# The last layer of a two-layer convolution block: a third tile of x by channels, asked for two units ahead, and residual rows asked for in their own unit

## The chip, the cores and the metric

The kernel runs on one core of one Trainium2 chip. A core has five engines that run beside each other, each with its own queue of instructions: TensorE (PE in the profile, its weight loads PEld) multiplies matrices, VectorE (DVE) and ScalarE (ACT) work on the elements, GpSimd (POOL) and SyncE (SP) do little here but issue DMA transfers. The engines wait for each other through semaphores. The metric is the time of one execution in microseconds (us); lower is better.

## What is computed

The input x has 48 channels of 256 x 256 pixels. The program runs two layers, each with a group normalisation `_gn` ahead of it and a residual sum behind it:

```python
# --- layer 0: attention over 4 x 4 patches, 8 heads ---
x = x + _L0_conv_ref(_gn(x), w_qkv, w_dw, temperature, w_proj)
# --- layer 1: this case is about this one ---
x = x + _L1_conv_ref(_gn(x), Ws, Hs, Cs, 64)

def _L1_conv_ref(x, Ws, Hs, Cs, window_size):
    B, C, H, W = x.shape
    ws = window_size                                   # 64
    xb = x.reshape(B, C, H // ws, ws, W // ws, ws)
    out = jnp.einsum('bcphqw,twW,thH,tcC->bCpHqW', xb, Ws, Hs, Cs)
    return out.reshape(B, C, H, W)
```

In layer 1 the picture is cut into 16 windows of 64 x 64 pixels. In each window, three terms t are added up, and in each term the data are multiplied by a 48 x 48 matrix over the channels, a 64 x 64 matrix over the columns of the window and a 64 x 64 matrix over its rows.

## The kernel before

Layer 0 takes the larger part of the program. It ends with a projection (lines 697 to 757), which writes its result with the residual added, 48 channels of 256 x 256 floats, to the tensor `x1s` in DRAM (L731), and works out the statistics that layer 1's normalisation needs. The normalisation is folded into the channel matrix `csn` and a bias `cbias`.

Layer 1 follows at L760. Its work is cut into eight units (L773): a unit is a strip of 64 rows by 128 columns, that is two windows side by side. The unit is worked through in these steps:

- `unit_load(u)` (L777) issues four DMAs on SyncE's queue. Two fetch the x tile `xq` ("lxq" in the profile, L784): channels on the partitions, once for the upper and once for the lower 32 rows of the strip. Two fetch the residual rows `rt` ("lrt", L787): image rows on the partitions, 24 channels each. Each of the four moves 768 KB in pieces of 512 bytes. Both kinds have two buffers (`bufs=2` of the pools `lx`, L760, and `lr`, L761).
- `over_c(u)` (L793) multiplies the x tile by the channel matrices, three image rows at a time, in 11 steps (L804: PSUM tile `pa`, two buffers). VectorE subtracts the bias and writes the product to `zt` ("lzt", L811). It is a generator: it stops after each step, and the caller decides when the next one is issued. A step takes a matmul for the upper and one for the lower half tile for each image row.
- `over_w(u, c0, c1)` (L819) multiplies by the column matrices for eight of the channels (L826: PSUM tile `pb`), and ScalarE copies the result to `yt` ("lyt", L833).
- `over_h(u, q)` (L836) multiplies by the row matrices and adds the three terms up in one PSUM tile `pc` (L843), which has a single buffer.
- `residual(u, q, pc)` (L852) lets VectorE add `pc` to the residual rows in place (L855). GpSimd then issues two stores of 256 KB from there to the output (L858). So a buffer of residual rows comes free when the last stores of its unit have landed.

The loop (L865 to L884) stands under `tc.manual_schedule()`: every engine gets its instructions in just the order in which the program text issues them. A unit has three parts q. Each part has two `over_w`, and behind each of them two steps of `over_c` of the unit after it. `over_h` runs one part late: that of part q of unit u is issued in the part that follows, and that of the last part in the first part of the next unit. `unit_load(u + 1)` stands at the head of unit u. SyncE computes nothing, so it takes the DMAs one after the other, as soon as the semaphores that each of them needs allow. A tile may be overwritten when all that read its buffer before have finished, and the framework puts the waits for that ahead of the DMA.

In the profile, TensorE's matmuls in fp32 are counted twice, so a call of `over_w` has 48 records where the text has 24.

Of the kernel before, what the change touches and what calls it, by code (L numbers as in the profile page):

```python
# [43 lines left out]
def conv_preact_kernel(  # L44
# [343 lines left out]
    with tc.tile_pool(name="xn", bufs=1) as xnp, tc.tile_pool(name="cst", bufs=1) as cst, tc.tile_pool(  # L388
        name="nps", bufs=2, space=PSUM
# [75 lines left out]
    with tc.If(nc.values_load(large) > 0):  # L465
# [8 lines left out]
        with tc.tile_pool(name="mk", bufs=NM) as mk, tc.tile_pool(name="mq", bufs=2) as mq, tc.tile_pool(  # L474
            name="mps", bufs=2, space=PSUM
# [23 lines left out]
    with tc.tile_pool(name="ahead", bufs=2) as ah, tc.tile_pool(name="ae", bufs=3) as ae, tc.tile_pool(  # L499
        name="asm", bufs=6  # L500
# [196 lines left out]
    with tc.tile_pool(name="pj", bufs=3) as pj, tc.tile_pool(name="pjs", bufs=1) as pjs, tc.tile_pool(  # L697
        name="pps", bufs=3, space=PSUM
# [58 lines left out]
        nc.vector.tensor_copy(cbias, pb1)  # L757


    with tc.tile_pool(name="lx", bufs=2) as lx, tc.tile_pool(name="lz", bufs=2) as lz, tc.tile_pool(  # L760
        name="lr", bufs=2  # L761
    ) as lr, tc.tile_pool(name="ly", bufs=4) as ly, tc.tile_pool(name="ps1", bufs=2, space=PSUM) as ps1, tc.tile_pool(
        name="ps2", bufs=2, space=PSUM
    ) as ps2, tc.tile_pool(name="ps3", bufs=1, space=PSUM) as ps3:
        wsb = lz.tile([128, T3, 128], F32, name="wsb", bufs=1)
        nc.vector.memset(wsb, 0.0)
        hsb = lz.tile([128, T3, WS], F32, name="hsb", bufs=1)
        for s in range(2):
            r = slice(s * WS, (s + 1) * WS)
            nc.scalar.dma_start(out=wsb[r, :, r], in_=Ws.rearrange("t w v -> w t v"))  # L770
            nc.scalar.dma_start(out=hsb[r], in_=Hs.rearrange("t h g -> h t g"))
        HW = WS // 2
        units = [(yw, xh) for yw in range(H // WS) for xh in range(2)]  # L773
        NQ = 3
        xqs, rts, zts, blks, parts = {}, {}, {}, {}, {}

        def unit_load(u):  # L777

            yw, xh = units[u]
            xcol = slice(xh * 128, (xh + 1) * 128)  # L780
            xq = lx.tile([64 + C, HW, 128], F32, name="lxq")
            for s in range(2):
                y0 = yw * WS + s * HW
                nc.sync.dma_start(out=xq[s * 64 : s * 64 + C], in_=x1s[:, y0 : y0 + HW, xcol])  # L784
            rt = lr.tile([128, NQ * 8, 128], F32, name="lrt")
            for s in range(2):
                nc.sync.dma_start(  # L787
                    out=rt[s * WS : (s + 1) * WS],
                    in_=x1s[s * 24 : (s + 1) * 24, yw * WS : (yw + 1) * WS, xcol].rearrange("c y x -> y c x"),
                )  # L790
            xqs[u], rts[u] = xq, rt

        def over_c(u):  # L793

            xq = xqs[u]
            zt = zts[u] = lz.tile([128, T3 * C, WS], F32, name="lzt")
            zv = zt.rearrange("p k (s y) -> p s y k", s=2)
            for y0 in range(0, HW, 3):
                n = min(3, HW - y0)
                pa = ps1.tile([128, 2, 512], F32, name="pa")  # L800
                for i in range(n):
                    for s in range(2):
                        r = slice(s * 64, s * 64 + C)
                        nc.tensor.matmul(  # L804
                            pa[:, s, i * T3 * C : (i + 1) * T3 * C],
                            lhsT=xq[r, y0 + i, :],
                            rhs=csn[r],
                            start=True,
                            stop=True,
                        )  # L810
                nc.vector.tensor_tensor(  # L811
                    zv[:, :, y0 : y0 + n, :],
                    pa[:, :, : n * T3 * C].rearrange("p s (y k) -> p s y k", y=n),
                    cbias.rearrange("p (u v k) -> p u v k", u=1, v=1).to_broadcast([128, 2, n, T3 * C]),
                    ALU.subtract,
                )
                yield

        def over_w(u, c0, c1):  # L819

            yt = ly.tile([128, T3, 512], F32, name="lyt")
            for t in range(T3):
                pb = ps2.tile([128, 4, 128], F32, name="pb2")
                for i in range(4):
                    for s, c in enumerate((c0, c1)):
                        nc.tensor.matmul(  # L826
                            pb[s * WS : (s + 1) * WS, i, :],
                            lhsT=zts[u][:, t * C + c + i, :],
                            rhs=wsb[:, t, :],
                            start=True,  # L830
                            stop=True,
                        )
                nc.scalar.copy(yt[:, t, :], pb.rearrange("p i x -> p (i x)"))  # L833
            return yt

        def over_h(u, q):  # L836

            pc = ps3.tile([128, 2, 512], F32, name="pc")
            for t in range(T3):
                for b in range(2):  # L840
                    for s in range(2):
                        r = slice(s * WS, (s + 1) * WS)
                        nc.tensor.matmul(  # L843
                            pc[b * WS : (b + 1) * WS, s, :],
                            lhsT=hsb[r, t, :],
                            rhs=parts[u, q][b][r, t, :],
                            start=(t == 0),
                            stop=(t == T3 - 1),
                        )
            residual(u, q, pc)  # L850

        def residual(u, q, pc):  # L852
            yw, xh = units[u]
            rv = rts[u][:, q * 8 : (q + 1) * 8, :].rearrange("p i x -> p (i x)")
            nc.vector.tensor_add(rv, pc.rearrange("p b n -> p (b n)"), rv)  # L855
            for s in range(2):
                c0 = s * 24 + q * 8
                nc.gpsimd.dma_start(  # L858
                    out=oc[c0 : c0 + 8, yw * WS : (yw + 1) * WS, xh * 128 : (xh + 1) * 128].rearrange("c y x -> y c x"),
                    in_=rts[u][s * WS : (s + 1) * WS, q * 8 : (q + 1) * 8, :],  # L860
                )

        with tc.manual_schedule():  # L865
            unit_load(0)
            for _ in over_c(0):
                pass
            late = None
            for u in range(len(units)):  # L870
                if u + 1 < len(units):
                    unit_load(u + 1)
                ahead = over_c(u + 1) if u + 1 < len(units) else iter(())
                for q in range(NQ):
                    parts[u, q] = []
                    for b in range(2):
                        c0 = b * 24 + q * 8
                        parts[u, q].append(over_w(u, c0, c0 + 4))
                        for _ in range(2):
                            next(ahead, None)  # L880
                    if late:
                        over_h(*late)
                    late = u, q
            over_h(*late)  # L884
# [41 lines left out]
```

## Time and profile before

| | us |
|---|---|
| median of 3 runs | 3835.93 (3830.28 to 3836.73) |
| the profiled execution | 3845.87 |
| its span, from the first to the last instruction | 3844.1 |
| first DMA of layer 1 to the end of the span | 3495.7 to 3844.1: 348.4 |

In layer 1, by the groups of instructions from 3495 us on:

| line, engine | what | busy us | count | mean ns |
|---|---|---|---|---|
| L826 PE | over_w | 147.9 | 2304 | 287 |
| L804 PE | over_c | 95.1 | 1024 | 333 |
| L843 PE | over_h | 67.3 | 576 | 598 |
| L811 DVE | bias, lzt | 136.3 | 88 | 1621 |
| L833 ACT | lyt | 84.3 | 144 | 586 |
| L855 DVE | residual | 29.4 | 24 | 1225 |

A line of the page or of an answer names the source line (L826), the engine, the operation, the tile written and the tiles read (`pb<-wsb,lzt`), and a count. "idle before" is time in which the engine stood still just ahead of the instruction, with the instruction or transfer that released it. The chain of waits goes back from the last instruction of the program, at each step to what released it or to the instruction before it on its engine; time that stands in the chain is time that sets the end. A DMA on SyncE's queue (SPq) is shown with the time of its issue, not with that of its data.

### The profile page before, as it was taken

What the parts mean: (1) busy time and instruction counts of PE and PEld (TensorE: products, weight loads), DVE (VectorE), ACT (ScalarE), POOL (GpSimd) and SP (SyncE); (2) the same over time, 40 slices, a digit from 0 to 9 for tenths busy, and PEclk for the clock granted to TensorE, in tenths of its full rate; (3) what the DMA queues carried; (4) which work ended last, traced back from release to release, by engine and by line L of the source; (5) the groups of instructions that cost most, each with busy time, mean ns of one, the idle gap of its engine ahead of it and who ended that gap; (6) DMA issues with size and microseconds to landing.
All of it is one profiled execution on the core that took longest, in us unless ns stands there. A gap on an engine that the chain in (4) does not pass through costs nothing.

```text
span 3844.1 us, 99863 instructions
## 1 busy us (share of the span) xinstructions
PE 3525.9 (92%) x44216; PEld 2927.6 (76%) x44216; DVE 2199.1 (57%) x3520; ACT 1717.9 (45%) x2668; POOL 583.3 (15%) x535
## 2 busy tenths in 40 slices
PE   1856999999999999999999999999999999755998
PEld 0324777788888888888888888888888888514776
DVE  5562776169727962994399359826972222365553
ACT  0223565555545544554455455545554444200222
POOL 0150212012201220221022112201220000000111
PEclk9877999999999999999999999999999999866999
DMA  6475676534523443444244325433542000598555
GB/s 142 153 163 144 178 196 179 175 109 117 119 81 101 119 110 87 104 120 98 83 117 115 94 81 128 111 88 92 128 113 75 24 18 22 116 238 141 111 105 100
DMA packets 280235, 441.66 MB, mean 115 GB/s; under 512 B 57354, under 2 KB 205082, under 8 KB 276336
## 3 DMA queue, kind: packets, MB, share of 16 engines
q1 hardware_dynamic: 225150, 260.52, 26.7%
q0 software_dynamic: 48896, 165.90, 19.2%
q10 hardware_dynamic: 5746, 8.73, 1.0%
q8 instruction: 351, 5.75, 0.6%
q14 instruction: 92, 0.75, 0.1%
HBM read 234.76 MB, written 199.95 MB: 113 GB/s over the span
## 4 chain that ended last, share of the span: by engine, by line
PE 73%; issue 10%; DMA 8%; DVE 2%; SPq 1%; POOL 0%; ACT 0%; POOLq 0%; ACTq 0%; DVEq 0%
PE big L339 32%; PE big L570 31%; DMA lxq<-x1s 3%; PE pb L826 3%; PE pa L804 2%; PE big L183 2%; DMA pot<-os__70 2%; PE pc L843 1%; DMA qkv<-o 1%; DMA pxt<-in_x_dram 1%; PE pst L524 1%; PE pt L587 1%; PE pn L253 1%; DMA xs<-in_x_dram 1%; DMA kt<-qkv 1%
## 5 line engine op out<-in xcount | busy, mean ns | idle before, releaser
L541 ACT ACTIVATE e<-big,nmx 128x1024 f32<-128x1024 f32 x1024 | 1144.0, 1117 | 846.2 <-PE big L339 636.4
L339 PE MATMUL big<-kt,qt 128*128 128x512 f32 x6144 | 1441.9, 394 | 57.9 <-DMA kt<-qkv 54.9
L570 PEld LDWEIGHTS big<-vn,e 128*64 128x64 f32 x32768 | 1364.8, 137 | 87.7 <-ACT e L541 45.1
L570 PE MATMUL big<-vn,e 128*64 128x96 f32 x32768 | 1422.7, 248 | 9.1 <-ACT ot L186 4.0
L339 PEld LDWEIGHTS big<-kt,qt 128*128 128x128 f32 x6144 | 1147.9, 189 | 322.0 <-issue 63.1
L581 DVE TENSOR_TENSOR oacc<-big,oacc 128x768 f32<-128x768 f32 x480 | 458.2, 955 | 708.7 <-PE big L570 708.7
L234 DVE SCALAR_TENSOR_TENSOR acc<-pad,dwt,acc 126x1024 f32<-126x1024 f32 x600 | 779.3, 1300 | 34.2 <-ACT acc L215 18.5
L292 POOL TENSOR_TENSOR ol<-o,oh 126x1024 fp32r<-126x1024 f32 x80 | 189.9, 2373 | 909.1 <-DVE ss L249 810.1
L554 DVE TENSOR_REDUCE zt<-zs 128x1 f32<-128x4 f32 x256 | 38.8, 152 | 368.5 <-ACT e L541 368.5
L811 DVE TENSOR_TENSOR lzt<-pa,cbias 128x864 f32<-128x864 f32 (+1 forms) x88 | 136.3, 1621 | 134.5 <-PE pa L804 134.5
L541 ACT ACTIVATION_READ_ACCUMULATOR e<-big,nmx 128x1 f32 x1024 | 196.3, 192 | 0.0
L833 ACT COPY lyt<-pb 128x512 f32<-128x512 f32 x144 | 84.3, 586 | 250.0 <-PE pb L826 250.0
L297 POOL DMA_DIRECT2D qkv<-o x80 | 101.0, 1262 | 567.8 <-DVE zu L556 348.7
L245 ACT ACTIVATE sq<-acc 126x1024 f32<-126x1024 f32 x75 | 79.3, 1058 | 171.7 <-issue 111.6
L279 DVE TENSOR_TENSOR o<-acc,y 126x1024 f32<-126x1024 f32 x75 | 149.4, 1992 | 11.0 <-DMA qkv<-o 11.0
L826 PEld LDWEIGHTS pb<-wsb,lzt 128*64 128x64 f32 x2304 | 132.1, 143 | 28.1 <-issue 21.1
L715 PE MATMUL pps<-pot,wp 96*96 96x512 f32 x128 | 77.9, 778 | 77.6 <-DMA pot<-os__70 77.6
L826 PE MATMUL pb<-wsb,lzt 128*64 128x128 f32 x2304 | 147.9, 287 | 1.3 <-issue 1.3
L186 ACT ACTIVATE ot<-big,bias 108x1024 f32<-108x1024 f32 x64 | 71.0, 1112 | 147.8 <-PE big L183 68.2
L804 PE MATMUL pa<-csn,lxq 48*128 48x144 f32 x1024 | 95.1, 333 | 33.9 <-DMA lxq<-x1s 32.6
L590 POOL DMA_DIRECT2D os__70<-oo x64 | 32.6, 514 | 615.4 <-ACT oo L589 615.4
L715 PEld LDWEIGHTS pps<-pot,wp 96*96 96x96 f32 x128 | 26.9, 218 | 128.0 <-issue 126.4
(115 smaller groups left out, 1897.6 us busy)
## 6 DMA issues: line engine op xcount, KB each, us to landing
pad<-t SPq DMA_DIRECT2D x80, 761.9 KB
qkv<-o POOLq DMA_DIRECT2D x80, 504.0 KB, 6.9
qkv<-oh POOLq DMA_DIRECT2D x80, 504.0 KB, 7.4
qkv<-ol POOLq DMA_DIRECT2D x80, 504.0 KB, 9.1
t<-ot SPq DMA_DIRECT2D x128, 217.7 KB
qt<-qkv SPq DMA_DIRECT2D x176, 96.0 KB
xs<-in_x_dram SPq DMA_DIRECT2D x128, 96.0 KB
os__70<-oo POOLq DMA_DIRECT2D x64, 192.0 KB, 2.8
```

The costliest lines, as they stand in the source:

```text
L234: nc.vector.scalar_tensor_tensor(self.acc, self.pad[:, dy : dy + KS, dx : dx + W], dwt[:, self.h, tap : tap + 1], self.acc, ALU.mult, ALU.add,
L279: nc.vector.tensor_tensor(self.o.rearrange("p (a b) x -> p a b x", a=KS), self.acc.rearrange("p a (x b) -> p a b x", b=KS), self.y.rearran ...
L292: eng.tensor_sub(self.ol, self.o, self.oh.bitcast(F32))
L297: nc.gpsimd.dma_start(out=qkv[self.h][i].rearrange("j (c k) n -> (j c) k n", k=KK)[:, :, px], in_=self.o if i == 2 else (self.ol if i else ...
L339: nc.tensor.matmul(ps[:, i, :], lhsT=qt[:, r, q0 : q0 + 128], rhs=kts[2 * j + i][:, r // 2, :], start=(r == 0), stop=(r == 2),)
L541: nc.scalar.activation(e[:, j * 1024 : (j + 1) * 1024], ps.rearrange("p a b -> p (a b)"), AF.Exp, bias=nmx[:, b : b + 1], accum_out=zs[:, ...
L570: nc.tensor.matmul(ps[p : p + 64, j // 4, j % 4 * HD : (j % 4 + 1) * HD], lhsT=e[:, mb * 128 + p : mb * 128 + p + 64], rhs=vn, start=(i == 0),
L581: nc.vector.tensor_add(oaccs[h, k], ps[:, :, : 4 * HD], oaccs[h, k])
L715: nc.tensor.matmul(ps[:, i : i + 2, :], lhsT=wp, rhs=ot[:, ki * KS + i : ki * KS + i + 2, :], start=True, stop=True,)
L804: nc.tensor.matmul(pa[:, s, i * T3 * C : (i + 1) * T3 * C], lhsT=xq[r, y0 + i, :], rhs=csn[r], start=True, stop=True,)
L811: nc.vector.tensor_tensor(zv[:, :, y0 : y0 + n, :], pa[:, :, : n * T3 * C].rearrange("p s (y k) -> p s y k", y=n), cbias.rearrange("p (u v ...
L826: nc.tensor.matmul(pb[s * WS : (s + 1) * WS, i, :], lhsT=zts[u][:, t * C + c + i, :], rhs=wsb[:, t, :], start=True, stop=True,)
```

## The change

`unit_load` is cut in two. `load_x(u)` fetches the x tile, `load_rows(u)` the residual rows. The pool of x tiles gets three buffers. Ahead of the loop the x tiles of units 0 and 1 are asked for; at the head of unit u the rows of that unit are asked for, and after them the x tile of unit u + 2.

```diff
-    with tc.tile_pool(name="lx", bufs=2) as lx, tc.tile_pool(name="lz", bufs=2) as lz, tc.tile_pool(
+    with tc.tile_pool(name="lx", bufs=3) as lx, tc.tile_pool(name="lz", bufs=2) as lz, tc.tile_pool(
...
-        def unit_load(u):
+        def load_x(u):
 
             yw, xh = units[u]
             xcol = slice(xh * 128, (xh + 1) * 128)
...
                 nc.sync.dma_start(out=xq[s * 64 : s * 64 + C], in_=x1s[:, y0 : y0 + HW, xcol])
+            xqs[u] = xq
+
+        def load_rows(u):
+
+            yw, xh = units[u]
+            xcol = slice(xh * 128, (xh + 1) * 128)
             rt = lr.tile([128, NQ * 8, 128], F32, name="lrt")
...
-            xqs[u], rts[u] = xq, rt
+            rts[u] = rt
...
-            unit_load(0)
+            for u in range(2):
+                load_x(u)
             for _ in over_c(0):
                 pass
             late = None
             for u in range(len(units)):
-                if u + 1 < len(units):
-                    unit_load(u + 1)
+                load_rows(u)
+                if u + 2 < len(units):
+                    load_x(u + 2)
```

What is computed stays the same; so does the order of the instructions on TensorE, VectorE, ScalarE and GpSimd.

## The prediction

> **What bounds the kernel now.** I read the page first, to see where the last layer lies, then the chain of waits over its end, the timeline of TensorE there, the timeline of SyncE's queue, and that queue's waits. The page says that TensorE is busy for 92% of the span, so a change to one layer can only win what TensorE stands still there. In the chain of waits (start in us, length in us, what) the last layer begins with the first x tile and then goes on so:
>
> ```profile
> 3496.13 13.98 DMA lxq<-x1s
> ...
> 3564.83 2.86 PE pb L826 x48
> 3567.69 1.67 PE pa L804 x24
> ...
> 3587.95 17.98 DMA lxq<-x1s
> ...
> 3605.97 3.25 PE pa L804 x22
> 3609.22 3.91 PE pb L826 x48
> ...
> 3629.00 17.38 DMA lxq<-x1s
> ```
>
> The reader is to see that up to 3584 the chain is TensorE alone, and that from there an x transfer of 17 to 19 us stands in it once per unit (five times: x tiles 3 to 7). On TensorE's own timeline (start, length, what, and in brackets the idle time before it and its releaser) these are the beginnings of units 1 and 2:
>
> ```profile
> 3564.76 2.93 PE L826 MATMUL pb<-wsb,lzt 128*64 128x128 f32 x48
> ...
> 3599.17 2.93 PE L826 MATMUL pb<-wsb,lzt 128*64 128x128 f32 x48
> 3602.03 0.51 PE L804 MATMUL pa<-csn,lxq 48*128 48x144 f32 x2
> 3605.97 3.25 PE L804 MATMUL pa<-csn,lxq 48*128 48x144 f32 x22 [3.43 <-DMA lxq<-x1s]
> 3609.15 3.98 PE L826 MATMUL pb<-wsb,lzt 128*64 128x128 f32 x48
> ```
>
> One matmul over channels (two records) runs on the half tile that has landed, then TensorE waits for the other half. Why the tile is late stands on SyncE's queue (start, length of the issues, tile):
>
> ```profile
> 3529.30 6.71 SPq L784 DMA_DIRECT2D lxq<-x1s  x2
> 3582.85 1.51 SPq L787 DMA_DIRECT2D lrt<-x1s  x2
> 3584.48 8.18 SPq L784 DMA_DIRECT2D lxq<-x1s  x2
> 3624.14 1.49 SPq L787 DMA_DIRECT2D lrt<-x1s  x2
> 3625.74 7.32 SPq L784 DMA_DIRECT2D lxq<-x1s  x2
> ```
>
> and in that queue's waits from 3520 on (waiter, releaser: us in total, times, longest):
>
> ```profile
> SPq L787 <- DMA out_dram<-lrt: 207.4, 13, 35.6
> ```
>
> The x tile of unit 3 is asked for only after the residual rows (lrt) of unit 2 have been issued, and those stand in the queue until the stores of unit 0, which read the same one of two buffers, have landed. Its own buffer had been free since over_c(1) ended near 3562. It then needs until 3605.9, while unit 2 wants it at 3602.
>
> [...] no L784 issue between 3536.0 and 3584.48, although its buffer was free. [...] the granted clock is 1.00 in unit 1 and 0.92 in units 2 to 5, and after the 3.43 us gap 22 matmul records take 3.25 us where 24 take 1.67, and the next 48 take 3.98 where they take 2.93.
>
> **The change, part by part.** A unit begins at the first matmul of its first over_w. From TensorE's timeline, units 1 to 7 begin at 3564.76, 3599.17, 3640.07, 3680.77, 3722.28, 3763.50 and 3806.91. Unit 1, which never waits, takes 34.41 us; TensorE is busy in all of it. Units 2 to 6 take 40.90, 40.70, 41.51, 41.22 and 43.41, together 207.74. Unit 7 has no over_c and no x to wait for.
>
> 1. *The x tile is asked for one unit earlier.* After the change SyncE's queue reads: x0, x1, rows 0, x2, rows 1, x3, rows 2, x4, rows 3, x5 and so on. Rows 2 still wait for the stores of unit 0 (3582.85, or 18.1 us into unit 1), and what goes out behind them at 3584.5 is x4 instead of x3. X4 lands after the same 21.4 us (3605.9 - 3584.5), some 41 us into unit 1. Unit 3 wants it 2.9 us after it begins: with units of 34.41, at 71.7. Margin about 30 us. X3 stands ahead of rows 2, waits only for over_c(0) (over at 3529.3), and is in long before 3602. So the wait in units 2 to 6 goes, with the cold matmuls after it: 207.74 - 5 x 34.41 = 35.7 us. As a check: the waits shown for the x tile between 3560 and the end are 20.0 us on TensorE in 5, and the cold stretch costs (3.25 - 22/24 x 1.67) + (3.98 - 2.93) = 2.8 each, 14 in all; 34.0 together.
>
> 2. *The rows are asked for in their own unit.* In the queue only their place against x changes: their wait for the stores of two units before ends at the same instant. Rows u land at the latest with the burst, 40 us into unit u-1, that is 5 us into unit u; the first residual wants them after two over_w pairs and over_h, 20.9 + 2.7 = 23.6 us into it. Cost nothing; the cover is 18 us at least.
>
> 3. *The third x tile.* 16 KiB more in each partition, no instruction. The buffer asked for in unit u held x of u-1, whose last reader ran in unit u-2. No new wait.
>
> 4. *The start.* Behind x0 now comes x1 and not rows 0; four issues as before, and x1 is wanted at 3535.9, the rows at 3554. X0 took until 3510.1. From 3496 to 3510.1 about 1.95 MB moved (the windows of DMA rate), of which x0 is 1.57; the other 0.38 is what followed it and the small weights. If none of that were in the way, x0 would be in 0.38 MB / 140 GB/s = 2.7 us sooner; if twice as much came between, 2.7 later. I take 0 and keep both ends.
>
> 5. *What is late next.* In a unit of 34.4 us VectorE has 11 x 1.62 + 3 x 1.22 = 21.5 us, ScalarE 18 x 0.586 = 10.5. The DMA share in units 2 to 5 was 0.62 to 0.67 of some 41.5 us, so about 27 us of a unit; it becomes 0.78. The burst (rows, x, and 0.99 MB of stores in 22 us) leaves 12 us free. If longer store landings (7.9 us in the burst against 4.5 over the layer) came into the period, I allow up to 1 us a unit, 5 in all; nothing as the value taken, since unit 1 ran at full speed beside half of such a burst.
>
> Sum against the profiled execution, 3845.87 (span 3844.1 and 1.8 around it): 3845.87 - 35.7 = 3810.2. The median shown is 9.9 lower, 3835.93; I take the same saving from it: 3800.2.
>
> **The rivals.**
> A, the forecast: stall gone, TensorE bound in all units: 3800.
> B, the DMA engines become the period. For: 27 us of 34 is much[...]. Against: all moved pieces are the same bytes, and the free 12 us. If units settle halfway, at 37.8, the gain is 5 x (41.55 - 37.8) = 18.7: 3817.
> C, the change doesn't do what it says, since x still stands behind waiting rows: for it speaks that this order of the queue stays; against, the unit that is gained. The same time as before: 3836.
> D, slower: the rows come too late for the residual. over_h has one PSUM tile, so a late row stops VectorE's add (L855), then over_h on TensorE, then all behind it. It would take rows that wait for the stores of the unit directly before: these land 18 us into the unit, plus 1.6 and 21.4 us, so 41, or 17 us after 23.6. Over six units that is 104 - 36 = 68 us more: 3904; rows that land first in the burst, after 13 of the 21.4 us by estimate, would be 9 us late, 54 - 36 = 18 more: 3854. I take the middle, about 3880. It decides from 36 / 6 = 6 us late per unit. Against it: lr keeps its two buffers, and 3582.85 is the stores of unit 0 for rows 2.
>
> **How the numbers follow.** A 0.85, of which a start that is some us better is part; B 0.07; C 0.04; D 0.04. A alone is 3800 with -2.7 to +2.7 for the start, up to +5 for the stores and about 4 either way for the run (the three before lie within 6.5 us): 3793 to 3812. To leave out no more than 2 in 10, and to reach towards B, I take 3792 to 3814. 0.2% is 7.7 us, about what a measurement of this kernel tells from no change; A and B lie beyond it: faster 0.92, same 0.04, slower 0.04.
>
> **What would show it.** Right: no DMA of x in the chain after the first; units 2 to 6 at 34.4 us each and a clock of 1.00 in them; x4's issue directly behind rows 2 near 3583, and unit 7 beginning near 3771. Wrong: idle time before pa L804 released by x (B, with x landing later than 30 us after its issue), or before lrt L855 released by the rows (D), or rows issued later than 18 us into the unit before their own.

## The result, and the profile after

| | before | after |
|---|---|---|
| median, us | 3834.38 (3829.95 to 3836.73) | 3806.55 (3802.84 to 3808.65) |
| ratio after / before, 95% interval | | 0.9921 (0.9908 to 0.9935) |
| the profiled execution, us | 3845.87 | 3807.91 |
| its span | 3844.1 | 3806.1 |
| first x issue to the end of the span (layer 1) | 348.4 | 314.1 |
| first over_w to the end of the span | 313.6 | 279.1 |

The kernel is faster by 0.8%, 27.8 us by the medians. In the profile, layer 1 is shorter by 34.3 us; the rest of the 38.0 us between the two spans lies ahead of it, where nothing was changed (the first x is asked for at 3495.74 before and at 3491.98 after). The two figures for the saving, 34 and 28, come back below.

The chain of waits of the changed kernel, over units 1 and 2 (start in us, length in us, what; its first line is the first x tile, ahead of unit 0):

```profile
3492.38 14.21 DMA lxq<-x1s
...
3562.32 2.86 PE pb L832 x48
3565.18 1.67 PE pa L810 x24
...
3596.73 2.86 PE pb L832 x48
3599.59 1.67 PE pa L810 x24
3601.26 2.86 PE pb L832 x48
...
3631.13 2.86 PE pb L832 x48
3633.99 1.67 PE pa L810 x24
```

No x transfer follows the first one. Units begin at 3562.3, 3596.7 and 3631.1, that is every 34.4 us. SyncE's queue of the same kernel (start, length of the issues, tile; L793 is the line of the rows now):

```profile
3525.68 10.71 SPq L793 DMA_DIRECT2D lrt<-x1s  x2
3536.50 7.68 SPq L784 DMA_DIRECT2D lxq<-x1s  x2
3580.29 1.50 SPq L793 DMA_DIRECT2D lrt<-x1s  x2
3581.89 8.51 SPq L784 DMA_DIRECT2D lxq<-x1s  x2
3614.88 1.52 SPq L793 DMA_DIRECT2D lrt<-x1s  x2
3616.50 7.51 SPq L784 DMA_DIRECT2D lxq<-x1s  x2
```

The rows of unit 2 are issued at 3580.29, 18.0 us into unit 1, as before the change, and x goes out directly behind them, as before. Only which x has changed: at 3581.89 it is that of unit 4, and that of unit 3 has left at 3536.50. The queue still waits for the stores, with nobody waiting for the queue (waiter, releaser: us in total, times, longest, from 3520 on):

```profile
SPq L793 <- DMA out_dram<-lrt: 168.1, 13, 30.3
```

The windows, one for each of units 1 to 4 (window in us, its length, busy time and count of PE, PEld, DVE, ACT, POOL, then granted clock, DMA share, GB/s):

```profile
3562.20:3596.70 34.50, 34.50 (x494) 26.15 (x490) 20.87 (x14) 10.56 (x18) 4.17 (x6) 1.00 0.63 116
3596.70:3631.10 34.40, 34.40 (x494) 26.11 (x490) 20.84 (x14) 10.55 (x18) 4.18 (x6) 1.00 0.77 140
3631.10:3665.50 34.40, 34.40 (x494) 26.10 (x490) 20.84 (x14) 10.56 (x18) 4.17 (x6) 1.00 0.76 128
3665.50:3699.90 34.40, 34.40 (x494) 26.10 (x490) 20.89 (x14) 10.56 (x18) 4.17 (x6) 1.00 0.81 149
```

TensorE is busy in all of each unit, at the full clock, and the DMA share has risen to 0.76 to 0.81 in units 2 to 4, where 0.62 to 0.67 stood in the longer units before.

### The profile page after: what moved, and what is told of

Same layout as the page of the kernel before. It is cut to its first block, busy times and chain, and to the rows that moved or that the text cites. A ratio compares the mean times of both kernels' runs of the same rounds, so it can differ in the third digit from the quotient of the medians.

```text
span 3806.1 us, 99864 instructions
## 1 busy us (share of the span) xinstructions
PE 3512.4 (92%) x44216; PEld 2911.7 (77%) x44216; DVE 2199.7 (58%) x3520; ACT 1718.5 (45%) x2668; POOL 584.2 (15%) x535
## 4 chain that ended last, share of the span: by engine, by line
PE 74%; issue 11%; DMA 6%; SPq 1%; DVE 0%; POOL 0%; ACT 0%; POOLq 0%; ACTq 0%
PE big L339 32%; PE big L570 31%; PE pb L832 4%; PE pa L810 2%; PE pc L849 2%; PE big L183 2%; DMA pot<-os__70 1%; DMA pxt<-in_x_dram 1%; PE pst L524 1%; PE pt L587 1%; PE pn L253 1%; DMA x1s<-pxt 1%; DMA t<-ot 1%; DMA kt<-qkv 1%; DMA lxq<-x1s 0%
## 5 line engine op out<-in xcount | busy, mean ns | idle before, releaser
L215 ACT ACTIVATE acc<-pad,dwt 126x1024 f32<-126x1024 f32 x75 | 85.3, 1137 | 72.7 <-DMA pad<-t 72.7
```

The source lines that it names most:

```text
L215: nc.scalar.mul(self.acc, self.pad[:, 0:KS, 0:W], dwt[:, self.h, 0:1])
```

## The experiments

All ratios are to the kernel before, on the same chip.

**Is it the third buffer or the order of the queue?** The new order lets x 3 stand ahead of rows 2. First, the changed kernel with two x buffers:

```diff
-    with tc.tile_pool(name="lx", bufs=3) as lx, tc.tile_pool(name="lz", bufs=2) as lz, tc.tile_pool(
+    with tc.tile_pool(name="lx", bufs=2) as lx, tc.tile_pool(name="lz", bufs=2) as lz, tc.tile_pool(
```

> The changed kernel with two x buffers instead of three; the order of the queue stays x0, x1, rows 0, x2, rows 1, x3, rows 2. Theory A, it is the order that counts: x3 now waits only for over_c(1), which ends near 3559, and stands ahead of rows 2, so it is asked for some 24 us earlier than before the change and lands near 3580, well before 3602. Then the time is that of the changed kernel, about 3806 us, within 4, and no x transfer stands in the chain after the first. Theory B, it is the third buffer that counts: x comes late again, about 3834 us.

Second, the third buffer alone in the kernel before (the same line, from 2 to 3, and the old calls):

> The kernel before with a third x buffer and nothing else; the order stays x2, rows 2, x3, rows 3. Theory A, order: x3 still stands behind rows 2, which wait for the stores of unit 0, so nothing changes: about 3834 us, within 4, and five x transfers stay in the chain. Theory B, buffer: about 3806 us.

Measured: two buffers in the new order 3810.35 us, ratio 0.9928 (0.9912 to 0.9944), as the changed kernel; three buffers in the old order 3842.35 us, ratio 1.0001 (0.9991 to 1.0011), as before. SyncE's queue of the two-buffer kernel shows why:

```profile
3553.05 1.10 SPq L784 DMA_DIRECT2D lxq<-x1s  x2
3573.78 1.50 SPq L793 DMA_DIRECT2D lrt<-x1s  x2
3587.46 1.07 SPq L784 DMA_DIRECT2D lxq<-x1s  x2
```

The x tile of unit 3 leaves at 3553.05, when over_c(1) has let go of its buffer, and the rows behind it at 3573.78, when the stores have landed; each waits for its own reason alone. And TensorE's timeline of the kernel with three buffers in the old order shows the old stall:

```profile
3606.31 0.51 PE L804 MATMUL pa<-csn,lxq 48*128 48x144 f32 x2
3609.50 3.24 PE L804 MATMUL pa<-csn,lxq 48*128 48x144 f32 x22 [2.68 <-DMA lxq<-x1s]
3612.67 4.13 PE L826 MATMUL pb<-wsb,lzt 128*64 128x128 f32 x48
```

So the order does it, and the third buffer by itself does nothing. It isn't needed with the new order either: the two-buffer kernel has no idle time released by x after the first tile. Its layer took 5 us longer than the changed kernel's in the profile (284.0 from the first over_w against 279.1); most of it lies in two units, beside two gaps in TensorE of 2.15 and 0.87 us that no semaphore explains (the last section comes back to them), and the medians do not separate the two kernels.

**Taking the wait away instead.** The kernel before, in its old order, with a third buffer of rows (`name="lr", bufs=3`):

> The kernel before with a third buffer of residual rows and nothing else. Theory A: the wait that held x up was that of the rows ahead of it in the queue; with three buffers rows 2 wait for nothing, rows 3 for the stores of unit 0, so x4 is issued some 40 us before it was: the stall goes, about 3806 us. Rival, the 17 to 19 us that an x transfer takes are the cause, whatever stands ahead of it: about 3834 us.

Measured: 3808.80 us, ratio 0.9925 (0.9910 to 0.9940). SyncE's queue of this kernel, with x 3, rows 3 and x 4:

```profile
3545.64 1.09 SPq L784 DMA_DIRECT2D lxq<-x1s  x2
3566.41 1.49 SPq L787 DMA_DIRECT2D lrt<-x1s  x2
3580.05 1.11 SPq L784 DMA_DIRECT2D lxq<-x1s  x2
```

The rows still wait for stores, but for those of the unit three before, and they have left before the x tile behind them has its buffer free. X 4 leaves at 3580.05, when over_c(2) has ended, some 40 us before it is wanted.

This run does not by itself exclude the rival, that the length of the transfer was the cause: here x goes out alone, and by the trace's DMA records it was in 12.5 us after its issue. The changed kernel excludes it. There x 4 leaves directly behind rows 2, as x 3 did before, and by the DMA records the two together take 21.1 us in both traces (3584.23 to 3605.37 before, 3581.67 to 3602.73 after), but TensorE does not wait. The length matters only together with a late start.

**The rows too late.** The changed kernel with one buffer of rows (`name="lr", bufs=1`), which is the slower case D of the prediction:

> The changed kernel with a single buffer of residual rows: rows u wait for the stores of unit u-1, as in the slower case D of the prediction, here from unit 1 on, seven units. The prediction's price for six units was 54 to 104 us above an unstalled layer: so 3860 to 3910 us, with idle time before lrt L861 released by the rows, and TensorE held up by the single pc tile. If rows are of no account for the end (their cover is larger than 18 us), the time stays near 3806.

Measured: 3836.73 us, ratio 0.9998 (0.9987 to 1.0009): 30 us above the changed kernel, and not the 54 to 104 that were expected. The rows came late, and so did x in two units; the waits of its engines from 3530 on:

```profile
DVE lrt L861 <- DMA lrt<-x1s: 48.7, 6, 16.8
PE pa L810 <- DVE lzt L817: 10.0, 7, 2.2
PE pc L849 <- DVE lrt L861: 6.9, 2, 5.5
PE pa L810 <- DMA lxq<-x1s: 4.2, 2, 3.1
```

In the chain of the same kernel the stores, the rows, the residual's add, the bias subtraction and over_c follow each other:

```profile
3580.69 0.69 POOL out_dram L864
3581.38 3.78 DMA out_dram<-lrt
...
3585.22 0.58 SPq L793
...
3585.85 11.24 DMA lrt<-x1s
...
3597.21 1.23 DVE lrt L861
3598.44 1.53 DVE lzt L817
...
3600.02 0.76 PE pa L810 x8
3600.78 4.38 PE pc L849 x24
```

The rows land 11.24 us after their issue, where the prediction had 13 to 21.4; two later x tiles of this chain, each asked for behind rows, stand in it with 17.72 and 18.21 us. VectorE waited 6.54 us for these rows. The late add holds up TensorE mostly by way of the bias subtraction behind it in VectorE's queue, and so over_c (10.0 us in 7 waits). Over_h waits for the add itself, by its single PSUM tile, in the last unit alone (5.5 us; the other wait of that kind, 1.4 us, stands at the end of the changed kernel too). And x, which stands behind the waiting rows in the queue, is late again in two units (4.2 us). The layer takes 310.2 us from its first over_w, 31.1 more than in the changed kernel: 19.7 by these waits, and the rest, 11.4 us, by their lengths in TensorE's timeline, in slow matmuls behind them. About 7 of the 31 us go to x and 24 to the rows. That the whole comes out even with the kernel before is chance.

**No x traffic at all.** In the changed kernel, units 3 to 7 read the x tiles that are there already; their x loads are left out:

```diff
-                if u + 2 < len(units):
-                    load_x(u + 2)
+                if u == 0:
+                    load_x(2)
+                elif u + 2 < len(units):
+                    xqs[u + 2] = xqs[u - 1]
```

> The changed kernel without the x loads of units 3 to 7: over_c of these units reads the three x tiles that are there, so nothing in them can wait for x, and the queue carries 10 transfers of 768 KB less. Output is not that of the reference. If the changed kernel has no stall left in timed runs either, this gives the same, 3806 within 3. If timed runs of the changed kernel still hold the 7 us that the saving fell short of the forecast, in a stall that the profile does not show, it gives about 3799.

Measured: 3802.40 us, ratio 0.9910 (0.9891 to 0.9929). The changed kernel, beside it on the same chip, took 3806.51 us, 0.9915 (0.9895 to 0.9934); in the profiles, the layer from its first over_w took 277.5 and 277.9 us. If the changed kernel still pays for its x loads, it is less than these intervals can tell; the 4 us between the medians lie between the two expectations.

**Before and after once more.** Was the first profile of before an odd one?

> The kernel before once more, for a second profile. The first profiled execution took 3845.87 us, 11.5 above the median of the timed runs, that of the changed kernel only 1.4 above. Theory P: the first profile of before was a slow one (its DMA transfers took longer, in the projection and for x): then this profile is near 3835, the first x is asked for some 3.5 us earlier in the span, and the five stalls are shorter, layer 1 taking some 342 us from the first x issue to the end and not 348. Theory Q: profiling itself lengthens stalls on DMA: then this profile is again near 3845, with 348 us in layer 1, and the timed runs near 3834.

> The changed kernel once more, beside the first-piece version on the same chip, and for a second profile: 3806 within 3, profile within 4 of it; layer 1 takes 314 us from the first x issue to the end of the span.

Measured: before 3840.49 us, its profiled execution 3847.53, and layer 1 took 349.2 us in it; after 3806.51, its profiled execution 3806.24, layer 1 311.8 us. The second profile of before came out as theory Q says, near 3845 with 348 us in layer 1, so the stalls of the first one were no accident. Whether they are shorter in timed runs was then tested in a way that needs no trace.

**Units of the steady state, timed.** The same units three times over:

```diff
-        units = [(yw, xh) for yw in range(H // WS) for xh in range(2)]
+        units = [(yw, xh) for yw in range(H // WS) for xh in range(2)] * 3
```

> The kernel before with its eight units of layer 1 worked through three times (24 units, the same output written three times). All but the first and the last unit of a pass are units in the steady state, so the time grows by 16 such units, and this holds in timed runs, in which no trace can be looked at. Theory Q, stalls are shorter in timed runs: the saving of 28 us over five stalled units says 34.4 + 28 / 5 = 40.0 us a unit, 640 us more than the kernel before, near 4477; the profile shows some 41.5 a unit. Theory P, the stalls are as long in timed runs as in the profile and the first profile differed in the stages before: 16 x 41.5 = 664 us more, near 4501.

> The changed kernel with its eight units worked through three times. With TensorE as the bound of each unit: 16 x 34.4 = 550 us more than the changed kernel, near 4357, in timed runs and in the profile alike. If a unit of the changed kernel takes longer in timed runs than in the profile (a stall that the profile does not show), it is more than that: the 7 us by which the saving fell short would be 1.4 a unit, 573 more, near 4380.

Measured: before 4500.28 us, after 4352.87. Over the same kernels with eight units (3838.46 on that chip; 3806.5, measured on other chips) this is 661.8 and 546.4 for 16 units, 41.4 and 34.2 us a unit in timed runs; in the profiles, from the first over_w to the end, it is (976.2 - 313.6) / 16 = 41.4 and (829.6 - 279.1) / 16 = 34.4. Between the two kernels of 24 units there are 21 stalled units: 147.4 / 21 = 7.0 us each in timed runs, and 5 x 7.0 = 35. A unit's stall is as long in timed runs as in the profile; theory Q falls.

**What lies ahead of layer 1.** The kernel before with the first unit only; the other seven are left out:

```diff
-        units = [(yw, xh) for yw in range(H // WS) for xh in range(2)]
+        units = [(yw, xh) for yw in range(H // WS) for xh in range(2)][:1]
```

> The kernel before with only the first of the eight units of layer 1: seven eighths of the output are left out. What is taken off is the stalled part. In the profile of before, layer 1 takes 313.6 us from its first over_w to the end of the span; with one unit that is about 37 (unit 7 took 37.2). If the timed runs of before hold the same, this is 277 us below before, near 3561 where before is near 3838. If the first pass stalls less in timed runs than in the profile, by the 6 us that the median's saving falls short of the units' 35, it is only 271 below, near 3567. A difference of 10 us in the stages ahead, as the profiles have them between executions of the same code, would hide either.

Measured: 3562.72 us (3551.38 to 3567.65), where before took 3835.12 on that chip: 272.4 less, between the two expectations, with a spread of 16 us in its own runs. This settles nothing.

**A version that beats both.** The changed kernel leaves one x transfer in the chain, the first, 14.21 us. It is fetched in four pieces of eight image rows, so that over_c(0) begins with the first:

```diff
-            for s in range(2):
-                y0 = yw * WS + s * HW
-                nc.sync.dma_start(out=xq[s * 64 : s * 64 + C], in_=x1s[:, y0 : y0 + HW, xcol])
+            n = HW // 4 if u == 0 else HW
+            for a in range(0, HW, n):
+                for s in range(2):
+                    y0 = yw * WS + s * HW + a
+                    nc.sync.dma_start(out=xq[s * 64 : s * 64 + C, a : a + n], in_=x1s[:, y0 : y0 + n, xcol])
```

> The changed kernel with the first x tile fetched in four pieces of 8 image rows, each for the upper and the lower half, so that over_c(0) can begin with the first piece. Over_c(0) takes 19 us, bound by VectorE; the tile takes 14.2 us to land whole. With the first piece in after some 5 us, over_c(0) begins 8 to 9 us sooner, and the whole layer with it: about 3798 us. If the small pieces are slower to land or over_c(0) then waits for each of them, 3803 or the same as the changed kernel, 3806.

> The changed kernel with the first x tile in four pieces, once more. Its first run was 19 us faster than the changed kernel where the profile of layer 1 shows 8 to 10. If the rest was variation of the stage before, this gives 3795 to 3800; if the pieces bring more in timed runs, again near 3788.

Measured: 3787.58 us, ratio 0.9865 (0.9844 to 0.9886), and the second time 3795.45, ratio 0.9885 (0.9870 to 0.9900). The chain of the first of them:

```profile
3495.51 4.17 DMA lxq<-x1s
...
3499.82 1.79 PE pa L812 x11
...
3501.63 1.62 DVE lzt L819
```

The first piece is there after 4.17 us, and over_c(0) never waits for the others. In the profiles layer 1 takes 303.7 and 303.2 us, 8 to 11 less than in the changed kernel's two. The medians show 19 and 11 less; the 8 us between two measurements of one kernel, on two chips, show how far a median of few runs can be trusted here.

## Why the prediction was right, and where its size was off

- *The x tile is asked for one unit earlier: 35.7 us.* Right in mechanism and, for the layer, in size: 34.3 us in the profile, 7.0 us for each stalled unit in timed runs. X 4 left behind rows 2, at 3581.89; units 2 to 6 take 172.1 us together, at a clock of 1.00, which is 35.6 less than before; unit 7 begins at 3768.85, and the forecast was near 3771 with a layer that began 3.8 us later. Unit 0 took 35.3 us and not 34.2, with two gaps of 0.67 and 0.81 us in it that have no releaser shown; they are about what the layer lacks to 35.6.
- *The rows cost nothing.* Right: VectorE's add waited for TensorE alone (39.3 us in 24 times, as before), never for rows. The experiment with one row buffer shows the cover: rows that leave one unit later cost about 24 us. It also shows that case D had its path only in part: TensorE waited for the bias subtraction behind the late add, for over_h's PSUM tile only in the last unit, and for x as well.
- *The third tile.* It was costed at nothing, and it is: but it also brings nothing. The prediction put the gain on x being asked for earlier and did not say that the order alone does it.
- *The start, 0 with 2.7 either way.* X 0 took 14.21 us from its issue and 13.98 before.
- *What is late next.* Nothing: TensorE. Case B, the DMA engines as the period, would have shown as TensorE waiting for x; at a share of 0.76 to 0.81 it does not wait. The prediction took this share for a share of the time, "about 27 us of a unit", and that reading was wrong: while the queue was full, the view of before gives shares over 1, as in this window of the burst (columns as above):

```profile
3588.00:3590.00 2.00, 2.00 (x34) 1.65 (x32) 1.42 (x2) 0.45 (x1) 0.00 (x0) 1.00 1.22 220
```

  Measured by 1.22, a share of 0.65 over 41 us is some 22 us of full load, by estimate, the length of the burst itself. Case B was further off than its argument had it.
- *The sum against the median.* Here the size was off: "I take the same saving from it: 3800.2", and the median is 3806.55. The term is the saving itself, 35.7, for which the medians show 27.8. The layer gave what was forecast; the two medians do not show all of it. Of the kernels without a stall, four measurements (the changed kernel twice, two x buffers, three row buffers) lie 27.8 to 30.7 us below before, and the one with no x loads 34.5. In the profiles, the first x of identical code was asked for anywhere between 3479.3 and 3499.7 us, because attention and projection, which the change does not touch, end at different times; that is more than the missing 5 to 7 us. But those four lie on one side. The two kernels of 24 units do not show a missing rest: they differ by 147.4 us in their medians and by 976.2 - 829.6 = 146.6 us in the profiles' layers. Where the 5 to 7 us of the eight-unit kernels go in timed runs stays open: the one-unit kernel was meant to tell, and did not.

## What to carry to other kernels

SyncE's queue held up what stood behind a waiting entry, however free its own buffer was: in the kernel before, x 3 left at 3584.48, 1.63 us after the rows ahead of it, with its buffer free since about 3562. So, before adding buffers, look in the queue for the entry whose wait ends last and for what it blocks, and put what waits for nothing ahead of it. Here a buffer added for what stood behind such an entry was worth nothing (ratio 1.0001), and one added for the entry that waited was worth as much as the new order (0.9925). And in a pipeline of equal units, check the price per unit by working through more units: timed runs then give it to some tenths of a microsecond, which the difference of two medians cannot.

## What the runs showed of the hardware that was not expected

- The length of a gap alone did not decide whether the matmuls behind it were slow. In the kernel before, the granted clock was 0.50 from 3604.70 to 3611.53, around the end of the gap of 3.43 us, and 1.00 ahead of and behind that stretch. In the kernel with one row buffer over_h was slow after a gap of 1.72 us: its 24 records took 4.46 us. In the kernel with three row buffers they took the usual 2.81 us after a gap of 2.31 us. TensorE's timelines of the two, in this order:

```profile
3600.02 0.76 PE L810 MATMUL pa<-csn,lxq 48*128 48x144 f32 x8 [1.72 <-DVE lzt L817]
3600.71 4.46 PE L849 MATMUL pc<-lyt,hsb 64*64 64x512 f32 x24
```

```profile
3662.43 0.88 PE L804 MATMUL pa<-csn,lxq 48*128 48x144 f32 x9 [2.31 <-issue]
3663.24 2.81 PE L843 MATMUL pc<-lyt,hsb 64*64 64x512 f32 x24
```

  In the kernel with two x buffers the gap of 2.15 us was followed by 2.81 us as well. Other gaps ahead of over_h in the kernel with one row buffer: behind 1.68, 1.97 and 2.24 us its 24 records took 4.50, 4.11 and 4.50 us, behind 0.91 and 1.23 us they took 2.81. What decides was not shown, and no run was made to test it.
- A short wait for data can be paid twice: between 1.6 us (behind the gap of 1.97 us just named) and 3.8 us (behind one of 4.72 us in the second profile of before) of slow matmuls were added to a gap, where they were slow. Of the 35.6 us that the five stalled units lost in the profile of before, 20.0 were waiting.
- In 15 places of layer 1, in eight of the traces, TensorE stood still for 0.2 to 2.3 us with no releaser that the trace shows (the 1.3 us ahead of the first over_w, which most traces have, are not among them). The two of the changed kernel, 0.67 and 0.81 us, lie beside transfers of x and rows: the DMA share was 1.19 and 1.27 in them. What TensorE waited for there was not shown.
